# Layer 0 self attention in nine score sets, output projection and statistics by chunk, layer 1 products one run later, mixes in halves

## The chip, the cores and the metric

The kernel runs on one core of a Trainium2 chip. Its engines work side by side: TensorE (PE; PEld are its weight loads), VectorE (DVE), ScalarE (ACT), GpSimd (POOL) and SyncE (SP), which issues transfers. Each works through a queue of its own in order and waits on semaphores for the others. The metric is the device time of one execution in microseconds. All data are fp32, and a matrix product of fp32 shows as two records of TensorE.

## The reference

A decoder of two layers on x of 4 batches, 1024 tokens and 256 features, with a context of 154 tokens per batch. Each layer has self attention, cross attention and a feed-forward part, each with a residual and a layer norm without weights:

```python
x = _layernorm(x + _L0_attn_ref(x, ...))                       # 16 heads of 16, causal
x = _layernorm(x + _L0_xattn_ref(x, ctx_1024, ctx_1024, ...))  # 16 heads of 64, no mask
x = _layernorm(x + _L0_ffn_ref(x, ...))                        # quantised, with a depthwise convolution
x = _layernorm(x + _L1_attn_ref(x, ...))                       # one head of 256, softmax over the queries
x = _layernorm(x + _L1_xattn_ref(x, ctx_1024, mask, ...))      # 16 heads of 16, masked keys
x = _layernorm(x + _L1_ffn_ref(x, ...))
```

The two parts that the change touches most:

```python
# layer 0 self attention
scores = jnp.einsum('bhqd,bhkd->bhqk', q * scale, k) + causal_bias
out = jnp.einsum('bhqk,bhkd->bhqd', jax.nn.softmax(scores, axis=-1), v)
out = out @ w_out.T + b_out                       # NaN becomes 0
# layer 1 feed forward; x_prev is x one token earlier, zero for the first
xr = mu_r * x + (1.0 - mu_r) * x_prev
xk = mu_k * x + (1.0 - mu_k) * x_prev
out = sigmoid(xr @ W_r.T) * (square(relu(xk @ W_k.T)) @ W_v.T)
```

## The kernel before

x of all four batches stays on the chip, in 8 chunks of 128 tokens per batch. Layer 0's self attention runs from the start to about 780 us; layer 0's cross attention and feed forward and layer 1's self attention follow to about 1845 us; layer 1's cross attention and feed forward (`cross_attention_and_feed_forward`) take the rest.

**Order.** In each stage calls are entered in a list with a time, `at(when, f, ...)`, and run in order of that time (`run_in_order`). A step has T = 20 units of time. TensorE's instructions, SyncE's transfers and the last operations of a layer norm are pinned to this program order; the order of the others on their engines comes from a scheduler. `layernorm` reads the statistics of 2 or 4 chunks (L136, L137), adds epsilon (L139), takes the power on POOL (L141), and leaves its last operations (L156 on VectorE, or L152 on ScalarE) as `pending` until 6 more events have run or `settle` is called because somebody needs x.

**Layer 0 self attention.** 16 steps, one for each group of four heads of a batch (four steps a batch), and one more to drain. To subtract the row maxima before the exponential, scores are computed twice. "A units" of step s are scores with the queries on partitions, reduced on VectorE to row maxima `nmp` (L319, and L335 for blocks on the diagonal). `shifted_queries`, at 20.3 of the step, reduces these once more to `nmt` (L344), turns nmt by eight transposes on TensorE (L351) and adds it to the queries, in rows of their own (`qs`, L355), so that the scores of the second kind come out shifted. These "B units" have the keys on partitions; ScalarE takes their exponential to tiles `p` (L385) and POOL clears what lies above the diagonal (L388). A call of `together` interleaves an A unit of step s with a B unit of step s−1; a unit has two heads, and 18 such calls stand at 1 to 18 of each step. B units go by sets: `b_sets` lists the pieces of (half of the queries, key chunk, column) that share a bank of PSUM. There are ten sets: 0 to 8 beside the A units, the tenth, a single piece of 256 columns, alone at 19. `weighted` multiplies p with v into one accumulator `acc` for each half of the queries, as the product of set i at 2i + 4.5, and for sets 8 and 9 at 20.1 and 20.4, around `shifted_queries`. `normalised` divides; after four steps `turned_back` transposes the batch's result, and `out_projected` applies the output weights to two chunks at once: four products, then three operations of VectorE on 512 columns (L474, L479, L480), the last two clearing NaN and adding to x. It stands at 11.5 and 15.5 of two steps per batch, counted as k7 and k8 from the batch's first step; the fourth batch's stands after its last step. PSUM has seven banks for everything ("s") and one for the accumulator.

**Layer 1 cross attention and feed forward.** Again 16 steps with the same scheme on 154 keys: `highest` (row maxima, three per step, at 0, 5 and 12), `shifted` (17), then in the following step `last_scores` (26 keys, at 2 and 3.5), `main_scores` (128 keys, at 8 and 14), `weighted` (at 13 and 20), and `normalised` another step on (3 and 4). Per batch, `turned` and `out_projected` follow, then `shifted_x` (x transposed into `fx`, L1433 and L1436), `mix` (ScalarE L1442 and VectorE L1443 over 1024 columns; two mixes of two halves of the features), `squared`, and `fed_forward` (tanh, product, sum on POOL at L1469, layer norm, output transfer). All products go through one helper whose line is L1166 in this stage, and L178 in layer 0's self attention.

Of the kernel before, what the change touches and what calls it, by code (L numbers as in the profile page):

```python
# [8 lines left out]
F32 = mybir.dt.float32  # L9
# [3 lines left out]
ALU = mybir.AluOpType  # L13
# [16 lines left out]
def decoder_kernel(ctx: ExitStack, tc: tile.TileContext, a: dict, out: bass.AP):  # L30
# [83 lines left out]
    def settle(b=None):  # L114

        for p in [p for p in pending if b in (None, p[1])]:
            pending.remove(p)
            p[2]()
# [10 lines left out]
    def layernorm(b, c0, n, scalar=False, then=None):  # L129
# [3 lines left out]
        st = small.tile([P, 4, nc.vector.BN_STATS_DIM], F32, tag="bnst", name="bnst", bufs=2)  # L133
        mv = small.tile([P, 4, nc.vector.BN_AGGR_DIM], F32, tag="bnmv", name="bnmv", bufs=3)
        for c in range(n):
            nc.vector.bn_stats(st[:, c, :], xb[:, c, :])  # L136
            nc.vector.bn_aggr(mv[:, c, :], st[:, c, :])  # L137
# [24 lines left out]
        pending.append([6, b, last_step])  # L162
# [10 lines left out]
    def self_attention(wk, pss, psa):  # L173
# [184 lines left out]
        b_sets = [(0, [(0, 0)]), (0, [(1, 0), (3, 384)]), (0, [(2, 0)])]  # L358
        b_sets += [(1, [(k, 0)]) for k in range(4)]
        b_sets += [(1, [(4, 0)]), (1, [(5, 0), (7, 384)]), (1, [(6, 0)])]  # L360
# [4 lines left out]
        def b_unit(s, i, pair):  # L365
            qh, pieces = b_sets[i]
# [3 lines left out]
            total = sum(width(qh, kc) for kc, _ in pieces)  # L370
            rounds = []
            for kc, c0 in pieces:
# [9 lines left out]
            def after():  # L382
                p = wk.tile([P, 2, 512], F32, tag="p", name="p", bufs=6)
                for g in range(2):
                    nc.scalar.activation(p[:, g, :total], t[g][:, :total], AF.Exp)  # L385
                for c0 in [c0 for kc, c0 in pieces if kc >= 4 * qh]:
# [19 lines left out]
        def weighted(s, i):  # L406
            b, t4 = divmod(s, 4)
            qh, pieces = b_sets[i]
            first, last = i in (0, 3), i in (2, 9)
# [3 lines left out]
            p2 = [pts.pop((s, i, pair)) for pair in range(2)]  # L413
            for kc, c0 in pieces:
                n = width(qh, kc)
                for g in range(4):
# [5 lines left out]
                        last,  # L422
# [37 lines left out]
        def out_projected(b, i):  # L460
            onT = ots[b, "n"]
            t = bank()
            for j in range(2):
                c = 2 * i + j
                for e in range(2):
                    mm(
                        t[:, j * E : (j + 1) * E],
                        onT[:, e, c * P : (c + 1) * P],
                        l0a_wo[:, e, :],
                        e == 0,  # L470
                        e == 1,
                    )
# [8 lines left out]
            if i % 2:  # L481
                layernorm(b, 2 * i - 2, 4)
# [1129 lines left out]
```

## Time and profile before

| | us |
|---|---|
| median of 3 runs | 2303.15 (2297.65 to 2305.23) |
| profiled execution | 2305.49 |
| its span | 2303.8 |
| TensorE busy | 2172.9 (94%) |
| VectorE busy | 1482.0 (64%) |
| ScalarE busy | 1127.3 (49%) |
| GpSimd busy | 507.7 (22%) |

The page gives busy times and shares of the span, the chain of work that ended last, and groups of instructions by line. The waits view lists, for an engine and a stretch of time, what its idle time ended on: total us, times, longest. A timeline line gives the start, the time until the end of a run of like instructions, engine, line, operation, tiles and shapes, the count, and in brackets the idle time before it with its releaser. A windows line gives the window, its length, the busy time (and count) of PE, PEld, DVE, ACT and POOL, then the granted TensorE clock as a share of full speed, the DMA share and GB/s.

In layer 0, the start of nmt's reduce (L344) marks the end of each step. These starts stand at 63.6, 104.2, 147.9, 192.1, 236.3, 279.9, 323.7, 373.0, 421.4, 463.9, 507.7, 557.8, 608.9, 653.5, 692.7 and 736.8 us: 44 us apart in most steps, 48 to 51 in those with an output projection of a batch.

### The profile page before, as it was taken

To read this page: it belongs to the slowest core of one execution; us is meant where nothing else is said; L and a number is where in the kernel's file an instruction comes from. 1 tells how busy PE (TensorE), PEld (TensorE's weight loads), DVE (VectorE), ACT (ScalarE), POOL (GpSimd) and SP (SyncE) were. 2 spreads that over 40 slices of the span, in tenths; PEclk is the share of its full clock that TensorE was granted. 3 is DMA by queue.
4 is the path that set the end of the run, shared out by engine and by line. 5 is a ranking of instruction groups with operands and counts; after the bars stand their busy time and mean duration, and the time that the engine had idled before them with its cause. 6 is when DMAs were issued, how large, how long until landed. Compare 5 with 4: busy or idle time off the path is not lost.

```text
span 2303.8 us, 38032 instructions
## 1 busy us (share of the span) xinstructions
PE 2172.9 (94%) x14228; PEld 1275.8 (55%) x14228; DVE 1482.0 (64%) x3223; ACT 1127.3 (49%) x2909; POOL 507.7 (22%) x1113
## 2 busy tenths in 40 slices
PE   7999999999999999999999998879989999999996
PEld 4444444454444556656556556556666755565645
DVE  4666666666666555558997887775873365555644
ACT  1455554554455465456656664444442234434354
POOL 1111111111112265444454432000000021111101
PEclk9999999999999999999999999989999999999998
DMA  3201100000000100000000000000000010010101
GB/s 89 55 7 33 39 23 15 10 15 15 6 15 1 38 1 19 1 1 1 1 1 1 33 1 21 1 1 1 1 1 1 2 20 15 10 32 11 28 1 37
DMA packets 24440, 34.78 MB, mean 15 GB/s; under 512 B 5952, under 2 KB 19648, under 8 KB 24256
## 3 DMA queue, kind: packets, MB, share of 16 engines
q1 hardware_dynamic: 22640, 31.20, 5.8%
q8 instruction: 113, 1.85, 0.3%
q10 hardware_dynamic: 1616, 1.16, 0.2%
q14 instruction: 71, 0.58, 0.1%
HBM read 15.56 MB, written 4.19 MB: 9 GB/s over the span
## 4 chain that ended last, share of the span: by engine, by line
PE 73%; DVE 19%; ACT 5%; issue 1%; POOL 1%; DMA 1%; SPq 0%; ACTq 0%; DVEq 0%; POOLq 0%
PE s L178 22%; PE t L568 15%; PE s L1166 10%; PE s L568 9%; PE acc L178 6%; DVE gt L917 4%; PE acc L1166 3%; PE t L752 2%; ACT u L727 2%; DVE bnst L136 1%; DVE x L156 1%; DVE nmp L319 1%; DVE nmx L723 1%; PE t L1075 1%; DVE ht L903 1%
## 5 line engine op out<-in xcount | busy, mean ns | idle before, releaser
L385 ACT ACTIVATE p<-s 128x512 f32<-128x512 f32 (+1 forms) x640 | 319.5, 554 | 296.3 <-PE s L178 293.6
L319 DVE TENSOR_REDUCE nmp<-s 128x1 f32<-128x512 f32 (+3 forms) x640 | 298.9, 524 | 156.4 <-PE s L178 156.4
L178 PE MATMUL s<-qs,kp 32*128 32x512 f32 (+3 forms) x1536 | 370.1, 531 | 2.7 <-DVE nmp L319 2.7
L178 PE MATMUL s<-kp,qp 32*128 32x128 f32 (+3 forms) x2304 | 330.2, 408 | 5.6 <-DVE nmp L319 3.5
L735 POOL TENSOR_SCALAR p<-u,rs 128x128 f32<-128x128 f32 x512 | 214.5, 437 | 290.5 <-DVE rs L731 196.1
L178 PEld LDWEIGHTS s<-kp,qp 32*128 32x128 f32 x2304 | 168.0, 188 | 142.9 <-issue 43.1
L388 POOL TENSOR_SCALAR_AFFINE_SELECT p<-p 128x256 f32<-128x256 f32 x256 | 100.6, 408 | 650.1 <-ACT p L385 650.1
L727 ACT ACTIVATE u<-s,nmx 128x154 f32<-128x154 f32 x512 | 192.0, 388 | 31.6 <-DVE nmx L723 27.1
L178 PEld LDWEIGHTS s<-qs,kp 32*128 32x128 f32 x1536 | 143.9, 186 | 65.0 <-DVE nmp L319 28.0
L141 POOL TENSOR_TENSOR rstd<-ve,neghalf 128x4 f32<-128x4 f32 (+1 forms) x56 | 55.3, 987 | 539.2 <-DVE ve L139 502.1
L178 PE MATMUL acc<-p,v 128*32 128x512 f32 (+3 forms) x1536 | 164.4, 508 | 1.1 <-ACT ot L427 0.8
L568 PEld LDWEIGHTS s<-kt,qt 64*128 64x128 f32 x1024 | 102.5, 188 | 71.6 <-issue 53.6
L568 PE MATMUL s<-kt,qt 64*128 64x154 f32 x1024 | 136.5, 316 | 0.5 <-ACT qt L709 0.3
L723 DVE TENSOR_REDUCE nmx<-s 128x4 f32<-128x616 f32 x128 | 101.2, 790 | 50.2 <-PE s L568 50.2
L568 PE MATMUL t<-xT,xw 128*128 128x512 f32 x256 | 122.4, 601 | 7.5 <-DVE xT L655 4.4
L1323 DVE TENSOR_REDUCE nmt<-s 128x3 f32<-128x462 f32 (+1 forms) x192 | 99.0, 579 | 46.4 <-PE s L1166 46.4
L917 DVE SCALAR_TENSOR_TENSOR gt<-ht,cw,gt 128x256 f32<-128x256 f32 x256 | 117.9, 501 | 6.6 <-ACT gt L913 5.5
L568 PE MATMUL t<-v,pt 128*128 128x256 f32 x512 | 117.7, 383 | 3.3 <-DVE pt L1076 2.9
L568 PE MATMUL s<-qt,xT 128*128 128x512 f32 x256 | 120.0, 613 | 0.0
L568 PE MATMUL t<-xw,ot 128*128 128x256 f32 x512 | 116.3, 381 | 3.6 <-ACT pr L756 1.9
L335 DVE TENSOR_REDUCE nmp<-s 128x4 f32<-128x512 f32 x128 | 82.6, 688 | 49.9 <-PE s L178 49.9
L568 PEld LDWEIGHTS t<-v,pt 128*128 128x128 f32 x512 | 97.1, 192 | 24.3 <-issue 6.2
(257 smaller groups left out, 3886.5 us busy)
## 6 DMA issues: line engine op xcount, KB each, us to landing
qp<-sq SPq DMA_DIRECT2D x128, 64.0 KB, 2.3
kp<-sk SPq DMA_DIRECT2D x64, 64.0 KB, 2.3
out_dram<-x SPq DMA_DIRECT2D x8, 512.0 KB, 2.9
x<-in_x_dram SPq DMA_DIRECT2D x3, 1024.0 KB, 5.4
wf<-in_L_ffn_w_dram SPq DMA_DIRECT2D x2, 1024.0 KB, 5.9
xw<-in_L_xattn_wk_dram SPq DMA_DIRECT2D x1, 1024.0 KB, 5.0
xw<-in_L_xattn_wq_dram SPq DMA_DIRECT2D x1, 1024.0 KB, 5.1
xw<-in_L_xattn_wv_dram SPq DMA_DIRECT2D x1, 1024.0 KB, 5.0
```

The costliest lines, as they stand in the source:

```text
L178: pe(nc.tensor.matmul(o, l, r, start=start, stop=stop))
L319: nc.vector.tensor_reduce(nmp[:, 2 * pair + g, qc, i : i + 1], t[g][:, c0 : c0 + n], AX.X, ALU.max)
L335: nc.vector.tensor_reduce(nmp[:, 2 * pair + g, q0 : q0 + 4, 0], t[g].rearrange("p (j n) -> p j n", j=4), AX.X, ALU.max,)
L385: nc.scalar.activation(p[:, g, :total], t[g][:, :total], AF.Exp)
L388: nc.gpsimd.affine_select(out=v, in_=v, compare_op=ALU.is_ge, fill=0.0, base=0, pattern=[[0, 2], [1, P]], channel_multiplier=-1,)
L568: pe(nc.tensor.matmul(o, l, r, start=start, stop=stop))
L723: nc.vector.tensor_reduce(nmx.rearrange("p i g -> p g i"), t, AX.X, ALU.max, negate=True)
L727: nc.scalar.activation(u[:, 2 * i + g, :], t[:, g, i, :], AF.Exp, bias=nmx[:, i, g : g + 1], accum_out=ssum[:, i, g : g + 1],)
L735: nc.gpsimd.tensor_scalar(p[:, h * P : (h + 1) * P], u[:, h, :P], rs[:, h : h + 1], 1.0, ALU.mult, ALU.mult)
L917: nc.vector.scalar_tensor_tensor(g, ht[:, i, k : k + N], cw[:, hc, k : k + 1], g, ALU.mult, ALU.add)
L1166: pe(nc.tensor.matmul(o, l, r, start=start, stop=stop))
L1323: nc.vector.tensor_reduce(nmts[s % 2][:, 3 * u : 3 * u + n, g, 17], ts[g][:, : n * LK].rearrange("p (c k) -> p c k", k=LK), AX.X, ALU.max, ...
```

## The change

- **Nine sets.** The tenth set's piece of 256 columns becomes a second round of set 2, whose bank has room for it; it belongs to the other half of the queries, so a piece now names its half. Its product goes to 10.6, after set 3's. The call at 19 is gone, and the product of set 8 stands at 20.4, after `shifted_queries`.
- **Output in eight places.** Layer 0's `out_projected` takes one chunk, with 256 columns on VectorE and a tile `y0` of its own. Batches 0 to 2 have it at 17.5 of k5, 15.5 of k6, 11.5, 15.5 and 17.5 of k7 and of k8.
- **Statistics by chunk.** `measured` takes a chunk's statistics where its x is finished; `layernorm` over four chunks finds them. `settle` can be limited to the four chunks that are needed.
- **Layer 1 products later.** `weighted` goes from 13 and 20 to 14.5 and 22.5, `normalised` from 3 and 4 to 3 and 5.4.
- **Mixes in halves.** `mix` works on 512 columns; for batches 0 to 2 the halves are spread over the time from `shifted_x` to `fed_forward`. The last batch has an order by halves of the tokens, and its final layer norms wait one event in place of six.

```diff
-    def layernorm(b, c0, n, scalar=False, then=None):
+    measures = {}
+
+    def measured(b, c):
+
+        if c % 4 == 0:
+            measures[b, c // 4] = small.tile([P, 4, nc.vector.BN_AGGR_DIM], F32, tag="bnmv", name="bnmv", bufs=6)
+        st = small.tile([P, nc.vector.BN_STATS_DIM], F32, tag="bnst", name="bnst", bufs=2)
+        nc.vector.bn_stats(st, xs[b][:, c, :])
+        nc.vector.bn_aggr(measures[b, c // 4][:, c % 4, :], st)
+
+    def layernorm(b, c0, n, scalar=False, then=None, wait=6):
...
-        pending.append([6, b, last_step])
+        pending.append([wait, b, last_step, c0])
...
-        b_sets = [(0, [(0, 0)]), (0, [(1, 0), (3, 384)]), (0, [(2, 0)])]
-        b_sets += [(1, [(k, 0)]) for k in range(4)]
-        b_sets += [(1, [(4, 0)]), (1, [(5, 0), (7, 384)]), (1, [(6, 0)])]
+        b_sets = [[(0, 0, 0)], [(0, 1, 0), (0, 3, 384)], [(0, 2, 0), (1, 6, 256)]]
+        b_sets += [[(1, k, 0)] for k in range(5)]
+        b_sets += [[(1, 5, 0), (1, 7, 384)]]
...
-        def weighted(s, i):
+        def weighted(s, qh, i, pieces, first=False, last=False):
...
-        def out_projected(b, i):
+        def out_projected(b, c):
             onT = ots[b, "n"]
...
+            t = bank()[:, :E]
+            for e in range(2):
+                mm(t, onT[:, e, c * P : (c + 1) * P], l0a_wo[:, e, :], e == 0, e == 1)
+            y = wk.tile([P, E], F32, tag="y0", name="y0")
+            nc.vector.tensor_tensor(y, t, bo2, ALU.add)
+
+            xb = xs[b][:, c, :]
             nc.vector.scalar_tensor_tensor(xb, y, 0.0, xb, ALU.max, ALU.add)
             nc.vector.scalar_tensor_tensor(xb, y, 0.0, xb, ALU.min, ALU.add)
-            if i % 2:
-                layernorm(b, 2 * i - 2, 4)
+            measured(b, c)
+            if c % 4 == 3:
+                layernorm(b, c - 3, 4)
...
-                at(t0 + (i // 2 + 7) * T + (11.5, 15.5)[i % 2] if b < 3 else t0 + 6 * T + i, out_projected, b, i)
+            for c in range(NC):
+                u = (117.5, 135.5, 151.5, 155.5, 157.5, 171.5, 175.5, 177.5)[c]
+                at(t0 + u if b < 3 else t0 + 6 * T + c, out_projected, b, c)
...
-            for i in range(10):
-                at((s + 1) * T + (2 * i + 4.5 if i < 8 else 20.1 + 0.3 * (i - 8)), weighted, s, i)
+            t0 = (s + 1) * T
+            at(t0 + 4.5, weighted, s, 0, 0, [(0, 0)], True)
+            at(t0 + 6.5, weighted, s, 0, 1, [(1, 0), (3, 384)])
+            at(t0 + 8.5, weighted, s, 0, 2, [(2, 0)], False, True)
+            for k in range(5):
+                at(t0 + 10.5 + 2 * k, weighted, s, 1, 3 + k, [(k, 0)], k == 0)
+            at(t0 + 10.6, weighted, s, 1, 2, [(6, 256)])
+            at(t0 + 20.4, weighted, s, 1, 8, [(5, 0), (7, 384)], False, True)
...
-            if s > 0:
-                at(s * T + 19, together, *[(b_unit, s - 1, 9, pair) for pair in range(2)])
...
-        def mix(b, i, e):
-            if e == 0:
+        def mix(b, i, e, q):
+            if (e, q) == (0, 0):
                 mixed[b, i] = wk.tile([P, 2, S], F32, tag=f"m{i}", name=f"m{i}", bufs=1)
-            m = mixed[b, i][:, e, :]
-            nc.scalar.activation(m, fx[:, e, 0:S], AF.Copy, scale=omu[:, e, i : i + 1])
-            nc.vector.scalar_tensor_tensor(m, fx[:, e, 1:], mus[:, e, i : i + 1], m, ALU.mult, ALU.add)
+            m = mixed[b, i][:, e, q * 512 : (q + 1) * 512]
+            nc.scalar.activation(m, fx[:, e, q * 512 : (q + 1) * 512], AF.Copy, scale=omu[:, e, i : i + 1])
+            nc.vector.scalar_tensor_tensor(
+                m, fx[:, e, 1 + q * 512 : 1 + (q + 1) * 512], mus[:, e, i : i + 1], m, ALU.mult, ALU.add
+            )
...
-            u = t0 + 6 * T + 5
-            for i in range(4):
-                e, q = divmod(i, 2)
-                at(u + 0.6 * i, shifted_x, b, e, q)
-                at(u + 10.3 + 6 * i, squared, b, e, q)
-                at(u + 37.2 + 8 * i, fed_forward, b, i)
-            for e in range(2):
-                at(u + 2.6 + 0.1 * e, mix, b, 1, e)
-                at(u + 2.8 + 0.1 * e, mix, b, 0, e)
+            u = t0 + 5 * T + 9
+            if b < NB - 1:
+                for i in range(4):
+                    e, q = divmod(i, 2)
+                    at(u + 0.1 + 0.6 * i, turned, b, e, q)
+                    at(u + 3.3 + 1.7 * i, out_projected, b, i)
+                    at(u + 16 + 0.6 * i, shifted_x, b, e, q)
+
+                    at(u + 18.4 + 2.4 * i, mix, b, 1, i % 2, i // 2)
+                    at(u + 26.3 + 6 * i, squared, b, i % 2, i // 2)
+                    at(u + 30.4 + 4 * i, mix, b, 0, i % 2, i // 2)
+                    at(u + 53.2 + 8 * i, fed_forward, b, i)
+            else:
+
+                for q in range(2):
+                    for e in range(2):
+                        at(u + 1 + 6 * q + e, turned, b, e, q)
+                        at(u + 4 + 6 * q + e, out_projected, b, 2 * q + e)
+                        at(u + 20 + 3 * q + e, shifted_x, b, e, q)
+                        at(u + 22 + 5.5 * q + 0.1 * e, mix, b, 1, e, q)
+                        at(u + 25 + 5 * q + e, squared, b, e, q)
+                        at(u + 27 + 6 * q + 0.1 * e, mix, b, 0, e, q)
+                        at(u + 28 + 6 * q + e, fed_forward, b, 2 * q + e)
...
-                at(t0 + 13 + 7 * q, weighted, s, q)
-                at(t0 + T + 3 + q, normalised, s, q)
+                at(t0 + 14.5 + 8 * q, weighted, s, q)
+                at(t0 + T + 3 + 2.4 * q if s < 4 * NB - 1 else t0 + T + (3, 12.5)[q], normalised, s, q)
```

## The prediction

> **What bounds the kernel now.** I read the page first (busy times, chain), then the waits of TensorE by stage, then the timeline where one step of layer 0's self attention ends, then windows around the places where the clock drops, then layer 1's mixing steps.
>
> The page:
>
> ```profile
> span 2303.8 us, 38032 instructions
> PE 2172.9 (94%) x14228; PEld 1275.8 (55%) x14228; DVE 1482.0 (64%) x3223; ACT 1127.3 (49%) x2909; POOL 507.7 (22%) x1113
> PE 73%; DVE 19%; ACT 5%; issue 1%; POOL 1%; DMA 1%; SPq 0%; ACTq 0%; DVEq 0%; POOLq 0%
> ```
>
> TensorE is the bound and nearly full: a gain must shorten its work or one of its few stalls, and a new stall adds its whole length. Its waits, first over 100 to 760 us (layer 0 self attention), then over 1845 to 2304 us (layer 1 cross attention and feed forward):
>
> ```profile
> PE s L178 <- DVE nmp L319: 5.6, 17, 0.7
> PE acc L178 <- ACT ot L427: 0.8, 1, 0.8
> PE s L351 <- DVE nmt L344: 0.7, 2, 0.3
> ```
>
> ```profile
> PE s L1166 <- ACT p L1349: 10.2, 4, 3.2
> PE s L1166 <- DVE m L1443: 3.1, 1, 3.1
> PE s L1433 <- DVE x L156: 2.6, 2, 2.4
> ```
>
> In layer 0 it loses 7 us of 660 and waits for the row maxima (nmt) twice only. In layer 1 four waits for the exponentials take 10.2. Now the end of one layer-0 step (about 325 us), TensorE and then VectorE:
>
> ```profile
> 322.12 1.06 PE L178 MATMUL acc<-p,v 128*32 128x512 f32 x8
> 323.11 0.71 PE L178 MATMUL s<-qs,kp 32*128 32x256 f32 x8
> 323.75 1.33 PE L178 MATMUL acc<-p,v 128*32 128x384 f32 x16
> 325.01 1.09 PE L351 MATMUL s<-ident,nmt 128*128 128x128 f32 x8
> 326.03 0.64 PE L178 MATMUL acc<-p,v 128*32 128x256 f32 x8
> ```
>
> ```profile
> 322.21 1.42 DVE L319 TENSOR_REDUCE nmp<-s 128x1 f32<-128x128 f32 x4 [1.57 <-PE s L178]
> 323.66 0.26 DVE L344 TENSOR_REDUCE nmt<-nmp 128x32 f32<-128x96 f32 x1
> ```
>
> After the last scores (322.12) TensorE does weighted set 7, the tenth set's scores (323.11) and weighted set 8, and only then the transposes of nmt at 325.01. nmt is ready at 323.92 plus some 0.15 of signalling, 324.07: it is hidden by those pieces of work. Last, the clock, in layer 0 beside an output projection and in layer 1 beside a mix:
>
> ```profile
> 549.80:553.20 3.40, 2.56 (x26) 1.63 (x22) 3.37 (x13) 1.46 (x3) 1.89 (x4) 1.00 0.01 2
> 553.24:556.65 3.41, 3.41 (x20) 1.47 (x18) 2.32 (x8) 1.09 (x2) 0.59 (x3) 0.50 0.00 0
> 1973.20:1976.60 3.40, 0.56 (x4) 0.29 (x2) 3.40 (x4) 3.37 (x4) 0.00 (x0) 1.00 0.00 0
> 1976.60:1980.00 3.40, 3.00 (x18) 1.32 (x18) 3.04 (x6) 1.80 (x4) 0.00 (x0) 0.50 0.00 0
> ```
>
> The columns are window, length, busy time of PE, PEld, DVE, ACT, POOL, then the granted clock. A stretch of 3.4 us in which VectorE is full and TensorE is not is followed by 3.4 or 6.8 us at half clock; in layer 0 2.56 busy of 3.40 was not enough to keep it, as many of its matmuls there use 32 rows of the array.
>
> The Trainium skill ("TensorE: Matmul & The Clock Gate", section "HAM oscillation — how this bites in real kernels") has the rule that TensorE's idle gaps over about 3.4 us bring the half clock. The row at 549.80 speaks against this as a sufficient reading: no gap there is that long. By the page alone the clock terms of layer 0 below would be nought, and the sum about 2 us lower.
>
> **The change part by part.** The profiled execution took 2305.49 us, 1.7 more than its span and 2.3 more than the median of the runs shown, 2303.15; changes are summed against its rows and applied to the median.
>
> *Nine sets*, 15 steps. Gone at the end of a step: the tenth set's scores (0.64), its products (0.57) and 0.18 of set 8 (1.25 becomes 1.07 of the same kind as the other sets): −1.39. Put back: the piece of 256 columns joins set 2, whose second unit goes from 1.48 (seen for it) to 1.90 (what a full second unit takes, limited by banks): +0.42; its products stand in mid-step behind set 3's: 0.57, of which 0.14 or less falls into a wait for banks: +0.43 to 0.57. New: weighted set 7 ends at 323.11 as before, but the transposes now follow at once and need nmt, 324.07: +0.96. Behind this wait on TensorE's queue stand set 8's products and the next step's scores. Sum +0.42 to +0.56, I take 0.45: **+6.8**. If nmt were never late it would be −0.5 a step (−7.6); if all of it and a bank wait showed, +0.8 (+12). ACT saves four exponentials a step, for which nothing waits. The joined set keeps its two tiles p to 10.6; six are in use then, freed by products that stand earlier in TensorE's order: nothing, and 0.6 (one exponential) a step if this is wrong.
>
> *Output projection by chunks.* Before, a pair of chunks costs VectorE three operations of 0.692 (L474, L479, L480) and twice 0.416 + 0.17 for statistics: 3.25; TensorE 1.9. A chunk alone: three of 0.424 (the row of 128x256 at L443), 0.416 and 0.17: 1.86; TensorE 0.96. Two per batch go into steps that had none, k5 at 17.5 and k6 at 15.5; k7 and k8 get three each in place of two pairs. What matters is VectorE's work between 15 and nmt.
> - k5: without a chunk the last pair takes 3.04 and its reduces run 3.14 to 4.56. With it VectorE ends the first unit's reduces at 2.59, the chunk at 4.45, the last reduces at 5.87: nmt 1.31 later, TensorE 0.06 more: +1.4.
> - k6: two units lie between the chunk and nmt: +0.2.
> - k7: two chunks late in the step (3.72 for 3.25) and the layer norm's four operations at L156 (4 x 0.43 and 0.17), which now fall before nmt, +2.3; less 1.4 for the smaller chunk at 11.5: +0.9.
> - k8: 0.47 more on VectorE, three TensorE pieces of 0.96 for two of 1.9 (−0.9): −0.2.
> Three batches: 6.9, less 0.7 since the last k8 is step 16 without row maxima: +6.2. Clock: the waits of 2.3 to 4.6 in k7 and k8 leave TensorE about as empty as at 549.80; I price a half-clock stretch of 3.4 to 6.8 us, worth 1.7 to 3.4, at 2.2 for the three k7 and 1.0 for two k8 (+8.6), and let the three of before (553, 604 and 734 us) go (−2.75, −2.75, −1.4): +1.7. The fourth batch's projection is the chain from layer 0's self attention to its cross attention (775 to 790 us, TensorE waits 4.75 there): 8 x 1.86 for 4 x 3.25: +1.9. Together **+9.8**. Bounds: +1.5 (no new half clock, the old ones gone) and +19 (3.4 at each of five).
>
> *Statistics by chunk* elsewhere: the same operations; the order of VectorE in 780 to 1845 us is nearly the one before, since they had already been placed as soon as a chunk was there: **0**, bounds ±2.
>
> *Products with v later* (layer 1). The products no longer follow the exponentials that they need so closely. In four steps (at 1880.5, 1895.8, 1934.2, 2221.9 us) they took 3.2 in place of 2.05, −1.2 each, less 1.2 for a later main score: −3.6. Against it: in two steps beside the feed forward (2021 to 2036, 2130 to 2145 us) the second main scores wait for banks whose reduce ends at 2034.93, because VectorE's queue stands behind statistics that wait for POOL (L1469); the products covered this (2032.21 to 2034.26) and no longer do: +1.9 each, and some 1.2 of clock: +5. **+1.4**, bounds −3.6 and +8.
>
> *Mixes in halves.* At 1972.01 four operations of 1.14 at L1442 (4.45) stand on ACT ahead of exponentials, TensorE idles 3.22 and then runs at half clock for 6.8 us (twice; 3.4 the third time). All gone: 3.2 and 3.4, 3.2 and 3.4, 3.2 and 1.7, −18.1. What is late next: three halves of the other mix on ACT (3 x 0.57) ahead of the second main scores' exponentials, and as many (3 x 0.64) on VectorE ahead of the last row maxima, some 1.4 of it on TensorE's path three times, and I keep half clock in two of the three: −18.1 + 4.2 + 6.8, near −7; **−6**, bounds −18 and 0.
>
> *The last batch's end.* The transposes of x still stand together in TensorE's order before the first squared half, so that start hardly moves: −1.2 for earlier products, −0.8 for four in place of eight last operations on ACT (4.04 for eight): **−2**, bounds −5 and +1.
>
> Sum +6.8 + 9.8 + 0 + 1.4 − 6 − 2 = **+10**: 2315.5 on the profiled execution, 2313 against the median. One measurement of this kernel tells 0.3% (7 us) from no change.
>
> **The rivals.**
> 1. *nmt is not late* (other side, faster). Place: the end of 15 steps of layer 0. For it: VectorE sat idle 1.57 before its last reduces, so it isn't behind. Against: those reduces can't start before the last scores end, and the 1.85 from there to nmt has only 1.00 of TensorE's work on top. Price: the 0.96 of each step, 14.4, and most of the 4 us of k5: the total is −8, 2295; with the mixes better than taken, 2285. It decides when the mean wait is under 0.3.
> 2. *The mixing stall and its half clock go entirely*: −18 in place of −6, total −2, about 2301: no measurable change. For it: a half is 0.57 in place of 4.45 in one piece. Against: the same work stays in the same step.
> 3. *Half clock at every step with an output projection*, +9 more, and the joined units dearer (+0.8): 2326. For it: 2.56 of 3.40 busy lost the clock. Against: the first batch's projections, at 365 us, did not lose it.
> 4. *The change of place does nothing*: the scheduler had already moved statistics, and may move mixes back; then the layer-0 terms stand alone: about 2319, inside my range.
>
> **How the numbers follow.** My sum (with 4) 0.46, from 2305 to 2321; rival 1 0.21; rival 2 0.19; rival 3 0.14. Slower by over 0.3% (2310): 0.38 of my sum's 0.46 and rival 3: 0.52. Within: 0.08 of mine and 0.13 of rival 2: 0.21. Faster: rival 1 and 0.06 of rival 2: 0.27. The range leaves out the end of rival 1 and the top of rival 3: 2289 to 2328; the likeliest alone 2305 to 2321.
>
> **What would show it.** Right: a wait of "PE s L351 <- DVE nmt L344" near 15 times 1 us in place of 0.7 in all, 2 to 4 in k5 and k7; no 3.2 at the mixes; a wait of about 2 for a bank after row maxima beside the feed forward; the stretch to 775 us longer by some 15, the one from 1845 us shorter by some 7. Wrong: no such wait (rival 1), or layer 1's stretch shorter by 15 and more (rival 2).

## The result and the profile after

The changed kernel took 2326.38 us (median of 6 runs, 2322.58 to 2330.46), the kernel before 2303.03 us (6 runs, 2297.65 to 2313.19): a ratio of 1.0101 with an interval of 1.0085 to 1.0118, so 23 us slower. The forecast was 2313, slower by 10: the direction held, the size was too small by more than half, and the time lies just inside the range. The profiled execution took 2322.58 us (span 2320.9), 17.1 us longer than that of before by its span. Of that, the trace accounts in three stages: 11.7 from the first to the last transposes of nmt in layer 0 (674.4 to 686.1 us), 4.6 from there to the first of layer 1's cross attention (1124.4 to 1129.0), 0.8 from there to the end (441.1 to 441.9). It was the fastest of the six executions, so some 6 of the 23 us are in no trace.

The page of the changed kernel, busy times and chain:

```profile
span 2320.9 us, 38012 instructions
PE 2159.2 (93%) x14196; PEld 1281.2 (55%) x14228; DVE 1495.9 (64%) x3287; ACT 1123.0 (48%) x2861; POOL 505.3 (22%) x1113
PE 71%; DVE 20%; ACT 6%; issue 1%; POOL 1%; DMA 1%; SPq 0%; ACTq 0%; POOLq 0%; DVEq 0%
```

TensorE is busy 13.7 us less in a span that is 17.1 longer: the change turned work into waiting. Where it waits, first over 100 to 760 us (layer 0's self attention), then over 1862 to 2321 us (layer 1's cross attention and what follows) (waits of TensorE: total, times, longest):

```profile
PE s L364 <- DVE nmt L357: 25.4, 15, 3.2
PE s L191 <- DVE nmp L332: 0.8, 4, 0.2
```

```profile
PE s L1444 <- DVE x L169: 5.6, 2, 3.2
PE s L1444 <- DVE nmt L1332: 4.4, 3, 1.5
PE s L1175 <- DVE nmt L1332: 2.9, 2, 1.5
PE s L1175 <- ACT ka L1467: 2.8, 1, 2.8
PE s L1175 <- ACT p L1358: 0.5, 1, 0.5
```

The wait for nmt is 25.4 us in place of 0.7. In layer 1 the four waits for exponentials (10.2) are down to 0.5, but waits for the row maxima's banks (7.3) and, at the last batch, for the squares (2.8) have come, and those for the last batch's layer norm are 5.6 in place of 2.6. The worst place in layer 0, the end of step k7 of the first batch, on VectorE and then on TensorE, and the clock there by windows:

```profile
372.13 0.41 DVE L476 TENSOR_TENSOR y<-s,bo 128x256 f32<-128x256 f32 x1
372.57 0.43 DVE L479 SCALAR_TENSOR_TENSOR x<-y,x 128x256 f32<-128x256 f32 x1
373.03 0.42 DVE L480 SCALAR_TENSOR_TENSOR x<-y,x 128x256 f32<-128x256 f32 x1
373.49 0.43 DVE L136 BATCH_NORM_STATS2 bnst<-x 128x6 f32<-128x256 f32 x1
373.95 0.18 DVE L137 BATCH_NORM_AGGREGATE bnmv<-bnst 128x2 f32<-128x6 f32 x1
374.05 1.39 DVE L332 TENSOR_REDUCE nmp<-s 128x1 f32<-128x128 f32 x4
375.36 1.37 DVE L169 TENSOR_SCALAR x<-x,bnmv,rstd 128x256 f32<-128x256 f32 x4
376.65 0.25 DVE L357 TENSOR_REDUCE nmt<-nmp 128x32 f32<-128x96 f32 x1
```

```profile
372.67 1.06 PE L191 MATMUL acc<-p,v 128*32 128x512 f32 x8
376.95 1.97 PE L364 MATMUL s<-ident,nmt 128*128 128x128 f32 x8 [3.22 <-DVE nmt L357]
```

```profile
368.80:372.20 3.40, 3.40 (x36) 2.29 (x34) 3.33 (x12) 1.44 (x3) 2.01 (x4) 1.00 0.14 23
372.20:375.60 3.40, 1.53 (x17) 0.37 (x12) 3.26 (x11) 1.08 (x2) 0.92 (x3) 1.00 0.33 58
375.60:379.00 3.40, 2.05 (x12) 1.72 (x16) 2.03 (x7) 0.00 (x0) 0.00 (x0) 0.51 0.01 1
```

The chunk placed at 17.5 (1.9 us) and the layer norm's four last operations (1.4) stand in VectorE's queue ahead of nmt; TensorE has only 1.0 us of products to do meanwhile, waits 3.22, and its emptied window is followed by half clock, so that the transposes take 1.97 in place of 1.09. Between 100 and 760 us the changed kernel has six such stretches, 27.3 us at half clock, the kernel before three with 17.1.

### The profile page after: what moved, and what is told of

The parts are those of the page before. It is cut to its first block, busy times and chain, and to the rows that moved or that the text cites. A ratio compares the mean times of both kernels' runs of the same rounds, so it can differ in the third digit from the quotient of the medians.

```text
span 2320.9 us, 38012 instructions
## 1 busy us (share of the span) xinstructions
PE 2159.2 (93%) x14196; PEld 1281.2 (55%) x14228; DVE 1495.9 (64%) x3287; ACT 1123.0 (48%) x2861; POOL 505.3 (22%) x1113
## 4 chain that ended last, share of the span: by engine, by line
PE 71%; DVE 20%; ACT 6%; issue 1%; POOL 1%; DMA 1%; SPq 0%; ACTq 0%; POOLq 0%; DVEq 0%
PE s L191 21%; PE t L575 15%; PE s L1175 10%; PE s L575 9%; PE acc L191 5%; DVE gt L925 3%; PE acc L1175 3%; DVE nmp L332 3%; PE t L759 2%; ACT u L734 2%; DVE x L169 1%; DVE nmx L730 1%; DVE bnst L136 1%; PE t L1083 1%; PE s L364 1%
## 5 line engine op out<-in xcount | busy, mean ns | idle before, releaser
L397 ACT ACTIVATE p<-s 128x512 f32<-128x512 f32 x576 | 312.8, 596 | 281.3 <-PE s L191 266.6
L191 PEld LDWEIGHTS s<-qs,kp 32*128 32x128 f32 x1536 | 151.3, 186 | 43.8 <-DVE nmp L332 19.3
L575 PE MATMUL t<-xT,xw 128*128 128x512 f32 x256 | 123.3, 604 | 10.2 <-DVE xT L662 6.6
```

Of the source, the lines that this page charges most:

```text
L191: pe(nc.tensor.matmul(o, l, r, start=start, stop=stop))
L397: nc.scalar.activation(p[:, g, :], t[g], AF.Exp)
L575: pe(nc.tensor.matmul(o, l, r, start=start, stop=stop))
```

## The experiments

All ratios are to the kernel before, timed on the same chip, with 95% intervals; a thousandth is 2.3 us. "Step" times are from one start of nmt's transposes to the next.

**The parts alone.** Four kernels are the kernel before with one part of the change each.

Nine sets, with the edits of the diff at `b_sets`, `b_unit`, `weighted` and their times:

```diff
+            at(t0 + 10.6, weighted, s, 1, 2, [(6, 256)])
+            at(t0 + 20.4, weighted, s, 1, 8, [(5, 0), (7, 384)], False, True)
...
-                at(s * T + 19, together, *[(b_unit, s - 1, 9, pair) for pair in range(2)])
```

> The kernel before with the nine score sets alone. Theory 1 (the wait for nmt that the tenth set had hidden): 15 new waits of TensorE for nmt of 0.9 to 1.0 us each, 14 us in all, less the shorter work at the end of a step: +4 to +8 us in all, seen as a step period of 44.1 to 44.4 us in place of 43.8. Theory 2 (the wait is hidden by less work at the step's end, and the time came from elsewhere): -5 to +2 us.

Measured: 1.0041 (1.0025 to 1.0056). The waits for nmt are 11.5 us, 14 times. But an ordinary step grew by 0.2 to 0.35 us only (43.97 in place of 43.77); the two steps with the first batch's output projection and the one behind them grew most, 49.78, 51.53 and 45.29 against 48.39, 48.36 and 43.52, with half clock at 367.5 and 418.7 us where there had been none.

Output projection by chunks in eight places, the statistics of four chunks still taken in the layer norm:

```diff
+                u = (117.5, 135.5, 151.5, 155.5, 157.5, 171.5, 175.5, 177.5)[c]
+                at(t0 + u if b < 3 else t0 + 6 * T + c, out_projected, b, c)
```

> The kernel before with layer 0's output projection by chunks in eight places alone, the statistics of four chunks still taken in the layer norm. Theory 1 (VectorE's chain after the last step, and POOL's power ahead of the masks of the last step, delay layer 0's cross attention): +8 to +14 us, of which +7 to +10 between 770 and 800 us. Theory 2 (only VectorE's chunks ahead of nmt in the steps with a projection): +4 to +8 us, all of it before 740 us and nothing over 2 us after it.

Measured: 0.9989 (0.9978 to 1.0000), no loss and at most a small gain, against both theories. Layer 0's steps together took 668.9 us in place of 674.4, with no half clock from 100 to 760 us. The end of the first step with a chunk at 17.5 in that kernel, VectorE and TensorE:

```profile
279.38 0.43 DVE L136 BATCH_NORM_STATS2 bnst<-x 128x6 f32<-128x256 f32 x1
279.94 1.38 DVE L319 TENSOR_REDUCE nmp<-s 128x1 f32<-128x128 f32 x4
281.36 0.26 DVE L344 TENSOR_REDUCE nmt<-nmp 128x32 f32<-128x96 f32 x1
```

```profile
278.54 1.07 PE L178 MATMUL acc<-p,v 128*32 128x512 f32 x8
280.72 0.69 PE L178 MATMUL s<-qs,kp 32*128 32x256 f32 x2 [0.48 <-DVE nmp L319]
281.34 1.07 PE L178 MATMUL acc<-p,v 128*32 128x384 f32 x16
282.34 1.09 PE L351 MATMUL s<-ident,nmt 128*128 128x128 f32 x8
```

Here nmt comes late too, at 281.62, 2 us after set 7's products, but TensorE has the tenth set's scores and set 8's products to do until 282.34. In this step the tenth set is what pays for the chunk.

Layer 1's products later, with 14.5 and 22.5 for `weighted`, 3 and 5.4 for `normalised`:

```diff
-                at(t0 + 13 + 7 * q, weighted, s, q)
+                at(t0 + 14.5 + 8 * q, weighted, s, q)
```

> The kernel before with layer 1's products with v later, alone. Theory 1: the first steps of the stage shorter by 3 to 4 us, the steps beside the feed forward longer by 2.5 to 3 us each (two of them inside the stage, one or two more near the end): 0 to +4 us in all. Theory 2 (only a gain): -4 us and no longer step beside the feed forward.

Measured: 1.0020 (1.0005 to 1.0035). The steps beside the feed forward took 24.3 and 24.2 in place of 22.1, a little less than the 2.5 to 3 that was expected. Not expected was that the three steps with a mix took 27.6, 27.7 and 27.7 in place of 26.4, 26.6 and 25.1. It is not more waiting: the waits for exponentials are 9.3 us in place of 10.2. The half clock in these steps is 10.2 us each, where before had 6.8, 6.8 and 3.4; half of the difference, 1.7, 1.7 and 3.4, is an estimate of its price, and covers the loss.

Mixes in halves, batches 0 to 2 spread as changed, the last batch's halves all at the old place:

```diff
-                at(u + 2.6 + 0.1 * e, mix, b, 1, e)
...
+                    at(u + 18.4 + 2.4 * i, mix, b, 1, i % 2, i // 2)
+                    at(u + 30.4 + 4 * i, mix, b, 0, i % 2, i // 2)
```

> The kernel before with the mixes in halves alone, spread over the step for batches 0 to 2, the last batch's halves all at the old place. Theory 1 (the stall turns into another: the first half's product on VectorE stands ahead of row maxima, and a nearly empty window of 3.4 us still comes): the three steps with a mix stay within 1.5 us of 26.4, 26.6 and 25.0, in all -3 to +4 us. Theory 2 (the stall is gone, and where the changed kernel lost it again it was the later products): the three steps shorter by 2 to 3 us each, in all -5 to -9 us.

Measured: 0.9949 (0.9931 to 0.9968), by theory 2 and the best of the parts. The three steps took 24.33, 22.92 and 24.08; the stage from its first transposes to the end 434.2 us in place of 441.1.

The four ratios add up to 1.000, the change made 1.010. So parts of it take each other's cover, or what none of the four contains (the statistics by chunk, the last batch's end) costs the rest. Four more kernels look into this.

**Pairs in layer 1.** The halves and the later products together, both edits as above:

> The kernel before with the mixes in halves and the later products together. Theory 1 (the later products take from the mixing steps the cover that the halves live on: the products of the step before stood between the two main scores): mixing steps of 25.0 to 27.0 us in place of the 24.3, 22.9 and 24.1 with the halves alone, steps beside the feed forward of 24.2 to 25.0 in place of 22.1, so -3 to +4 us against the kernel before and +7 to +13 us against the halves alone. Theory 2 (the parts add): -11.2 and +4.3, -7 us against the kernel before.

Measured: 0.9992 (0.9984 to 1.0001). Theory 1: the steps with a mix took 25.1, 26.7 and 25.7, those beside the feed forward 25.1 and 24.1. The later products cost 0.43% where the halves are, against 0.20% alone; that they cost more in company is not shown, as each figure is good to 0.15 or 0.2% only, and the stage from layer 1's first transposes of nmt on is longer by 6.9 us with the halves and by 6.4 without. The waits of TensorE in the halves alone, then with the later products:

```profile
PE s L1166 <- DVE nmt L1323: 3.1, 3, 1.1
PE s L1166 <- DVE m L1443: 1.0, 1, 1.0
```

```profile
PE s L1433 <- DVE nmt L1323: 4.4, 3, 1.5
PE s L1166 <- DVE nmt L1323: 2.9, 2, 1.5
```

The first half of a mix stands on VectorE ahead of row maxima, whose banks TensorE needs next: 3.1 us in three places with the old order of products, 4.4 at the three mixes and 2.9 more beside the feed forward with the new. The products that had stood between were part of the cover. But at the mixes the waits grew by some 1.3 us in all, and the three steps by 6.2. In the second, which grew most, half clock is nearly all of it: 6.8 us in place of none. What the first and the third lost (0.8 and 1.7) beyond their waits was not found. In the traces of the other kernels with halves the three steps together have 14 to 20 us of half clock with the later products and 7 to 14 with the old ones.

**Statistics by chunk, with the eight places**, `measured` wherever a chunk of x is finished:

```diff
+            measured(b, c)
+            if c % 4 == 3:
+                layernorm(b, c - 3, 4)
```

> The kernel before with the eight places and the statistics by chunk everywhere. Theory 1 (with its statistics taken early, the layer norm's eight last operations come ahead of the copies of transposed x between the layers, and TensorE idles some 3 us longer there, with half clock after it): +3 to +8 us against the eight places alone, between 765 and 800 us. Theory 2 (statistics by chunk cost nothing): within 2 us of the eight places alone, 2301.

Measured: 0.9992 (0.9978 to 1.0007), the same as without. The trace does show what theory 1 says: ahead of layer 0's cross attention TensorE waits 6.62 us for xT in place of 3.20. But the whole stretch up to layer 1's cross attention was not longer (1122.4 us against 1126.0), because less half clock fell into it (49.2 us in place of 63.3). The runs do not separate the two. Less half of its half clock, an estimate, the stretch is 3.4 us longer here, and 2.3 and 4.9 longer in two of the three other pairs of kernels below that differ in it by the statistics alone (0.2 shorter in the third). So theory 1's few us are likely, and not shown by the runs.

**The nine sets with a cover put back.** The larger piece of set 8's products goes ahead of nmt's transposes:

```diff
-            at(t0 + 20.4, weighted, s, 1, 8, [(5, 0), (7, 384)], False, True)
+            at(t0 + 20.1, weighted, s, 1, 8, [(5, 0)])
+            at(t0 + 20.4, weighted, s, 1, 8, [(7, 384)], False, True)
```

> The kernel before with the nine sets, but the larger piece of the last set's product (384 columns, some 0.8 us) moved ahead of the transposes of nmt, over the wait. Theory 1 (the whole loss of the nine sets is TensorE's uncovered wait for nmt): waits for nmt of at most 0.3 us in place of 0.8 each, 8 to 12 us less than the nine sets alone, so 2300 to 2304. Theory 2 (the loss is in the joined set and the products in mid-step): 2309 to 2313 as with the nine sets alone.

Measured: 1.0035 (1.0020 to 1.0049): theory 1 fell as it was stated. The waits for nmt are gone (1.5 us in all), and nothing was gained: an ordinary step is 44.17 long, longer than with the wait. TensorE at the end of such a step:

```profile
320.00 0.39 PE L178 MATMUL s<-qs,kp 32*128 32x128 f32 x4
320.31 2.69 PE L178 MATMUL acc<-p,v 128*32 128x512 f32 x16
322.93 1.09 PE L351 MATMUL s<-ident,nmt 128*128 128x128 f32 x8
```

The sixteen records of products last 2.69 us without a bracket. Set 7's take 1.0 by themselves, and 384 columns some 0.8: there are 0.8 us left in which the second batch of products waits for its own exponentials. ScalarE ends these at 321.63, and the mask follows on POOL. The view of waits does not show this wait, but it is as long as the one for nmt. So the end of this step is two chains of about the same length, to nmt and to the last exponentials with their mask, and neither can cover the other. Of the work that had stood there, only the tenth set's scores depended on neither.

**The two parts without a loss**, eight places and halves:

> The kernel before with the eight places and the mixes in halves, without the other parts: the two that were no loss alone. If they add: 2290 (-13 us). If what the eight places gained was only the phase of half-clock windows: 2292 to 2296.

Measured: 0.9960 (0.9947 to 0.9973), −9 us, or 2294 from 2303: the second expectation, and no better than the halves alone. That the eight places gain anything of their own is not shown.

**Nine sets and eight places together**, both edits as above:

> The kernel before with the nine sets and the eight places together. Alone they took +0.41% and -0.11%. Theory 1 (they share one cover: the tenth set's scores hid the chunks' VectorE work ahead of nmt, so that with nine sets each chunk late in a step is paid on TensorE): +14 to +22 us (0.6 to 1.0%), waits for nmt of 20 us or more in place of 11.5 and 2.3, steps with a chunk at 17.5 longer by 1 us and more. Theory 2 (they add): +5 to +9 us.

Measured: 1.0076 (1.0059 to 1.0092), by theory 1; the sum of the parts would be 1.0030. Waits for nmt are 25.4 us, to the digit those of the changed kernel, and the steps are those of the changed kernel within 0.1 us. Layer 0's slowdown is this pair.

**Taken out of the changed kernel.** First the nine sets:

> The changed kernel with the ten sets put back, all else as changed. Theory 1 (nine sets cost more beside the eight places than alone): 14 to 22 us less than the changed kernel, so within 0.4% of the kernel before on either side. Theory 2 (nine sets cost what they cost alone): 7 to 11 us less, so +0.5 to +0.7% against the kernel before.

Measured: 1.0000 (0.9987 to 1.0013), theory 1: within the changed kernel the nine sets cost 1.0%, all of the slowdown. Then the later products:

> The changed kernel with layer 1's products with v at their old times (13 and 20, division at 3 and 4), all else as changed. Theory 1 (the later products take the cover from the halved mixes and from the steps beside the feed forward): 7 to 12 us less than the changed kernel, with mixing steps of 23 to 24.5 and steps beside the feed forward of 22.1. Theory 2 (the later products cost only what they cost alone): 3 to 5 us less.

Measured: 1.0076 (1.0053 to 1.0099), 6 us less than the changed kernel, between the two theories (the intervals of the two overlap; in the traces layer 1 is 4.5 shorter), with steps of 24.3, 22.9 and 22.9 at the mixes and 22.1 beside the feed forward, as theory 1 has it.

**No chunk at 17.5.** Nine sets and eight places again, with other times:

```diff
-                u = (117.5, 135.5, 151.5, 155.5, 157.5, 171.5, 175.5, 177.5)[c]
+                u = (125.6, 135.5, 145.6, 151.5, 155.5, 165.6, 171.5, 175.5)[c]
```

> The nine sets and the eight places with no chunk at 17.5 of a step: chunks at 5.6 and 15.5 of k6, 5.6, 11.5 and 15.5 of k7 and of k8 (none in k5). Theory 1 (what costs is VectorE's work for the chunk that stands right ahead of nmt): 5 to 10 us less than nine sets and eight places as changed, waits for nmt of 12 to 15 us. Theory 2 (the chunks cost wherever they stand, since VectorE has no slack in a step): within 3 us of it.

Measured: 0.9979 (0.9968 to 0.9991), 24 us less than with the places as changed. That is more than theory 1 had, and faster than the kernel before. VectorE and TensorE at the end of the same step k7, and the waits over 100 to 760 us:

```profile
363.86 1.37 DVE L156 TENSOR_SCALAR x<-x,bnmv,rstd 128x256 f32<-128x256 f32 x4
371.46 1.42 DVE L319 TENSOR_REDUCE nmp<-s 128x1 f32<-128x128 f32 x4 [0.36 <-PE s L178]
372.91 0.26 DVE L344 TENSOR_REDUCE nmt<-nmp 128x32 f32<-128x96 f32 x1
```

```profile
373.31 1.06 PE L351 MATMUL s<-ident,nmt 128*128 128x128 f32 x8 [0.69 <-DVE nmt L344]
```

```profile
PE s L351 <- DVE nmt L344: 13.5, 15, 2.0
```

VectorE waits for TensorE here (0.36) and no longer the other way round for long. Two things have left the place ahead of nmt: the chunk, and the layer norm's four last operations (L156), which stand at 363.86, as the fourth and the eighth chunk now come one place earlier. Waits fall by 11.9 us, and half clock between 100 and 760 us from 27.3 to 3.4 us, worth up to another 12, some of it the same time. The steps from first to last take 667.3 us in place of 685.9.

The same edit alone in the changed kernel:

> The changed kernel with one edit: no chunk at 17.5, places as in the run with early chunks. Theory 1 (the chunk right ahead of nmt, met by the nine sets' missing cover, is most of the slowdown): 15 to 22 us less than the changed kernel, -0.1 to +0.3% against the kernel before. Theory 2 (the nine sets themselves and layer 1 are most of it): 2 to 8 us less, +0.6 to +0.9%.

Measured: 1.0007 (0.9993 to 1.0022), 0.94% or 22 us less: with three chunks per batch taken from the end of a step to its first third or to the next step, and the layer norms' last operations moved along with them, the changed kernel is not told from the kernel before. Chunks and layer norms were not moved apart. Step k5 of the first batch has a chunk at 17.5 and no layer norm, and takes 45.3 in place of 43.8 for it; k7 has both, and takes 48.7 in place of 46.5.

**The best of it.** Nine sets, early places, halves:

> The kernel before with the nine sets, the output projection by chunks at the earlier places (none at 17.5) and the mixes in halves; layer 1's products, the statistics and the last batch's end as before. If the gain of the early places (-0.21%) and of the halves (-0.51%) add, as they lie in different stages: 2283 to 2289 against 2300, -0.5 to -0.75%. If one of them was phase of the half-clock windows: -0.2 to -0.5%.

Measured: 0.9927 (0.9913 to 0.9941), as the two gains added would be. The same with ten sets:

> The same with the ten sets. Theory 1 (with nothing of VectorE's right ahead of nmt, the wait of the nine sets, 0.8 a step, costs as much as the tenth set's own work): within 3 us of the kernel with nine sets. Theory 2 (nine sets cost wherever the chunks stand, 0.4% alone): 6 to 10 us faster than with nine sets.

Measured: 0.9918 (0.9904 to 0.9931), 2284.7 us: theory 1. Where no chunk is late the nine sets cost 2 us, which the runs do not tell from nothing; in the traces layer 0's steps are 2.5 longer with them. The kernel with nine sets, early places and halves, now with the last batch's end as changed:

> The first kernel of this call with the last batch by halves of its tokens and its final layer norm after one event, as in the changed kernel. My estimate of the end was -2 us: between -4 and 0 against the kernel without it. Rival (the halves leave TensorE emptier ahead of the last products, so that half clock lasts longer): +1 to +4.

Measured: 0.9957 (0.9945 to 0.9970), so the new end costs 0.30%, 7 us. The waits of TensorE from 2160 us on, without it and with it:

```profile
PE s L1426 <- DVE x L156: 3.6, 2, 2.4
PE s L1159 <- DVE m L1436: 1.5, 1, 1.5
```

```profile
PE s L1426 <- DVE x L156: 5.6, 2, 3.2
PE s L1159 <- ACT ka L1449: 2.8, 1, 2.8
```

Half by half, TensorE waits for each half's layer norm and for each half's squares; all at once, the other half's work had covered these. That is 3.3 us of the 7. The rival has its share too: in layer 1 the trace has 34.8 us of half clock in place of 25.1, 6.8 of it from 2273.9 on, at the wait for the squares; half of the difference, 4.9, is an estimate of its price. The halves of the tokens and the earlier layer norm were not tried apart. Last, the kernel with ten sets, with the later products in the first five steps of the stage alone:

```diff
-                at(t0 + 13 + 7 * q, weighted, s, q)
+                at(t0 + (14.5 + 8 * q if s < 5 else 13 + 7 * q), weighted, s, q)
```

> The kernel with ten sets, early chunks and halved mixes (0.9918 of the kernel before), with layer 1's products later in the first five steps of the stage alone, where no mix and no feed forward stands. Theory 1 (the later products gain where nothing else hangs on their old place, as the first steps showed, -4 us together): 0.988 to 0.991 of the kernel before. Theory 2 (the gain moves into a wait of the next steps): 0.991 to 0.993.

Measured: 0.9907 (0.9889 to 0.9925), 2280.54 us, the fastest of all. Its five first steps take 94.1 us in place of 96.6, but its interval overlaps that of the kernel without this edit, which ran on another chip, so the gain is seen in the trace and not shown by the runs.

## Why the prediction was right or wrong, point by point

- **Nine sets, +6.8.** Right in size: 9 us alone. The wait is there, 0.79 in the step that the prediction showed (predicted 0.96, with 0.15 from nmt to the transposes, where the trace has 0.06), and so are the joined set (+0.44) and the products in mid-step (+0.44). Wrong in place: an ordinary step lost 0.2 to 0.35 rather than 0.45, and the rest came in steps with a projection, by half clock. "If nmt were never late it would be −0.5 a step" fell: with nmt on time the last exponentials are late instead.
- **Output projection, +9.8.** Right beside the nine sets (1.0041 to 1.0076, 8 us), and its trace: k5 was priced +1.4 and shows 45.3 against 43.8 with early places. Beside ten sets the same part is −2.5 us by its run, hardly told from nothing. The prediction made its sum in one order only and did not say that the price holds only without the tenth set. Its bound of +1.5 was in this sense not a bound. Three of its small figures do not come out of its own rows: the terms for k8 (+0.47 and −0.9) make −0.4 and not −0.2, the bounds come to +1.2 and +18, and TensorE's waits from 775 to 790 us are 3.9 and not 4.75. Nothing hangs on them.
- **Half clock, +1.7 of it.** Too low: 27.3 us in place of 17.1 in layer 0 is +5. Rival 3 named 2326 and half clock at every step with a projection. The changed kernel's trace has it at six places in layer 0, two for each batch, and the time came out at 2326. That is luck: rival 3 put some 30 us on layer 0, whose two parts took 17.5 together (1.0076); the rest of the 23 came from elsewhere.
- **Statistics by chunk, 0 ± 2.** Holds in the runs (0.9992 against 0.9989), though the wait for xT ahead of layer 0's cross attention doubled (3.20 to 6.62), and the traces, less half of their half clock, have 2 to 5 us more in three pairs of four. "The order of VectorE in 780 to 1845 us is nearly the one before" did not hold there: eight operations of the layer norm came ahead of the copy. The +1.9 for the fourth batch's projection left this out: the changed kernel took 9 us more than before between its last transposes of nmt and layer 0's cross attention, 4.7 of it from the start of the projection on, and some 3.4, an estimate, by the 6.8 us of half clock at 751 us.
- **Products with v later, +1.4: this is a step that failed.** The gain in the first steps (−2.5 with this part alone, predicted −3.6) and the loss beside the feed forward (+2.1 each, predicted 1.9 and some clock) came. What was left out is the steps with a mix, +1 to +3.8 each: the term looked at each place where TensorE stalled before and at the feed forward, but not at the mixes, whose new halves stand in the same place. There the runs show 10.2 us of half clock in each of the three steps with this part alone (17.0 in all before), and beside the halves waits of up to 1.5 for a bank, with 3.4 to 6.8 us of half clock in each. Alone it is +4.6 us, beside the halves +10, and 6 when taken out of the changed kernel.
- **Mixes in halves, −6.** Alone −12 us by the runs and −6.9 in the trace; the mechanism was right. In the changed kernel the steps with a mix took 26.6, 25.0 and 26.7 against 26.4, 26.6 and 25.1: nothing was left. The prediction added −6 and +1.4, −4.6; the two parts together made −2 by the runs and nothing in layer 1's stage of the trace (441.1 us in both).
- **The last batch's end, −2: the other step that failed.** It is +7. The working saw the start of the squared halves and four operations on ACT; it did not ask what each half waits for when the other half's work no longer stands between (3.3 us of waits), nor what the clock does then (9.7 us more of half clock).
- **The rivals.** Rival 1 (nmt not late) is out, by 25.4 us of waits. Rival 2 (the mixing stall and its half clock go entirely, −18) is out as well: without the later products the waits for exponentials do go (10.2 to 0.5), but 3.1 of waits for banks and some half clock stay, and the halves make −6.9 in the trace and −12 in the runs. Rival 4 (the change of place does nothing) is out: the halves alone made −0.51%, the early places took 24 us off the pair of nine sets and eight places.

Put together by the runs: layer 1 was forecast at −6.6 and is +5 (halves and later products −2, the end +7). This is 12 of the 13 us that the forecast was short of; layer 0 with +16.6 was about right. Two direct differences agree, statistics included: all the rest of the change made +0.25% (6 us) on top of nine sets and eight places, and +0.28% on top of nine sets and early places. The two profiled executions alone would not have shown it: layer 1 is 0.8 us longer there. Single executions scatter by more than some of these terms, so a sum of this kind, in medians, is good to a few us only.

The Trainium skill's rule ("TensorE: Matmul & The Clock Gate", "HAM oscillation — how this bites in real kernels"), no idle gaps over about 3.4 us, would have let all this pass: in the windows above 1.9 us of a 3.22 us gap fell into one window, and half clock began before the gap was over. The row of before, 2.56 busy of 3.40, was the better guide, though not a sure one: the last section has the same work without half clock after it.

## What to carry to other kernels

Work that is taken off the bounding engine may be the cover of a dependency; before removing it, ask what the engine does in its place until the next input is there, and whether that too depends on something late. Price parts of a change in each other's company: two parts that use the same slack cost together what neither costs alone (0.76% here against a sum of 0.30%), and the cheapest repair was not to undo either but to move three small pieces per batch, and a layer norm's end with them, away from the critical hand-over. Ahead of such a hand-over an engine's queue should hold nothing that can wait.

## What the runs showed of the hardware that was not expected

A wait of TensorE on products can leave no idle time in the profile: sixteen records of products that take 1.8 us elsewhere (1.0 and some 0.8) showed 2.69 as one run without a bracket, and only the end of the exponentials on ScalarE, and of their mask, told why. And half clock falls differently in executions of the same code: layer 0's step k7 of the second batch took 51.09 us in one kernel and 48.38 in another whose layer 0 is the same, with 6.8 us of half clock from 553 us in the one and none in the other:

```profile
549.80:553.20 3.40, 2.57 (x29) 1.69 (x26) 3.37 (x14) 1.27 (x3) 2.09 (x4) 0.97 0.01 2
553.20:556.60 3.40, 3.40 (x19) 1.42 (x18) 2.31 (x8) 1.09 (x2) 0.58 (x3) 0.50 0.00 0
```

```profile
546.10:549.50 3.40, 2.57 (x30) 1.69 (x26) 3.37 (x14) 1.23 (x3) 2.12 (x4) 1.00 0.01 2
549.50:552.90 3.40, 3.40 (x43) 1.47 (x42) 3.05 (x10) 1.72 (x5) 0.83 (x3) 1.00 0.00 0
```

The first pair of windows is the kernel with the later products alone, the second the same work in the one with halves and later products, which came to it 3.7 us earlier: 2.57 us of TensorE busy in 3.40 both times, and half clock after it in one only. Half clock lasts 3.41 us or a multiple of it wherever these traces show it in the middle of a kernel. Where the same busy work lies against such a grid of time seems to decide it; that was not tested by itself.

Busy time alone does not tell either. In the trace of before from 100 to 2290 us, cut into pieces of 3.41 us from the start of half clock at 553.24 us both ways, 22 pieces at full clock have 1.5 to 2.6 us of TensorE busy and no product of 32 rows, and 20 of them are not followed by half clock; of five pieces with 2.4 to 2.6 us busy, mostly with products of 32 rows, four are. That fits the prediction's reading of the row at 549.80. One of the 20, with less than half of it busy:

```profile
1389.50:1392.90 3.40, 1.52 (x8) 1.30 (x8) 3.40 (x8) 2.79 (x13) 0.56 (x2) 1.00 0.04 10
1392.90:1396.30 3.40, 3.40 (x17) 2.05 (x17) 2.83 (x7) 2.11 (x9) 2.13 (x6) 1.00 0.00 0
```
